# Four graph layers on one core: the column lists of layer 0 made tile by tile, more listed tiles there, and three edge sums moved to layer 2

## The chip, the cores and the metric

One Trainium2 chip, of which the kernel uses one core. The metric is device time in microseconds of one execution, given as the median of several runs. Before the change the three runs took 2618.31, 2622.95 and 2624.23 us, so the median is 2622.95.

## What is computed

The inputs are node features x (4096 x 256) and an adjacency matrix adj (4096 x 4096, float32), whose entries thin out towards high row and column numbers: entry (i, j) is non-zero with a probability that falls with the square root of i times j, and the diagonal is full. Four layers follow one another, each with a residual and a layer norm:

```python
x = ln(x + adj @ (x * W))                 # layer 0
x = ln(x + L1(x, adj))                    # layer 1: two steps of top-p attention beside R = rownorm(adj + I)
x = ln(x + L2(x, adj))                    # layer 2: softmax of adj * score over the neighbours, times x
neighbour_edges = einsum('ij,ji->i', adj, adj)
x = ln(x + concat(x, adj @ x, neighbour_edges) @ weight + bias)   # layer 3
```

The edge sum of layer 3 for a row i, the sum over j of adj[i, j] * adj[j, i], depends on adj alone, so it can be worked out at any time before layer 3.

## The kernel before

**Tiles.** There are 32 row tiles of 128 rows. Rows of low number have neighbours nearly everywhere, so tiles 0 to 2 (DENSE = 3) are always multiplied with all 32 column blocks. For the others the kernel finds which columns of adj hold anything for the tile, and makes a list of these columns, in blocks of 128. CAPS (line 66) says how many blocks each tile's list may have: 7, 7, 6, 7, 5, 6, 5, 5, 5, 5, 5, 5, 6 for tiles 3 to 15, then 5 for eight tiles and 4 for eight, 146 in all. A listed block costs a gather of 128 rows by GpSimd (an indirect DMA, line 393), wherever it is used: features in each of the layers, and once the pair of adj and its transpose, 128 rows of 256 numbers.

**Layer 0** (its pieces from line 476, its loop from line 619). SyncE's queue loads the whole adjacency, 256 KB panels for tiles 0 to 15 (dense_0, line 547) and 512 KB parts for tiles 16 to 31 (find_0, line 560). VectorE reduces each of these to `seen` (lines 552 and 563), which says for each row and column block whether a column is used. TensorE multiplies the panels of tiles 0 to 15 with x (line 550). Once all of tiles 16 to 31 are seen, list_columns makes one list for all sixteen: eight lists of a sixteenth of the columns each, by rounds of MAX8 and MATCH_REPLACE (lines 347 and 349) over 512 elements. Then a tile is started every third turn (L_EVERY); listed_0 gathers its pairs and its rows of x, multiplies them (line 593), forms the edge products on VectorE (lines 595 and 402), and writes the blocks of the tile to HBM (pk) for later layers. The same loop slips in edges_0, the edge sums of tiles 0 to 2, from 2 MB loads on ScalarE's queue and products of 2048 columns (line 614). The end of a tile, out_0, is cut in seven pieces (rone, y, st, mv on VectorE, rs on GpSimd, xi on VectorE, transposes and projections on TensorE, copies and DMAs on ScalarE), and move_ends lets one piece go per turn, two apart from the tile ahead.

**Layer 1, first step.** A plan written out by hand (PERIOD and AT) orders the pieces of each tile's attention (narrow). It makes its own short lists of large attention weights, tile by tile (lines 1212 to 1254). Beside it r_stream multiplies the listed blocks with the layer's features: the tiles 16 to 31 first, whose blocks are in pk, then tiles 3 to 15, whose pairs have to be gathered here and whose edge products are formed here (line 1352). The second shared list, for tiles 3 to 15, is made here too. **Second step:** for each tile, a search on VectorE and ScalarE over 4096 attention weights (lines 781, 787, 862, 868, 910, 914), a dense product with the features (line 237), and the listed blocks beside it (line 1087).

**Layers 2 and 3** are two calls of product: the panels of the hub tiles (0 to 2 in layer 2, 24 panels; 0 to 5 in layer 3, 48) are mixed with the pieces of the listed tiles from 31 down. In each turn it fetches up to three pieces ahead (loads on SyncE's queue, gathers on GpSimd), weighs the piece of the next turn (ScalarE exponentials at line 1593 and a VectorE product at line 1594, in layer 2 only), multiplies this turn's piece (line 1659), and moves the ends of finished tiles by a step.

**Order.** Inside these parts the program's order on TensorE, ScalarE, VectorE and GpSimd is that of the code (`manual_schedule(engines=everything)`); SyncE's queue is ordered by the framework's scheduler. Each engine works its queue in order. If a check at the end finds that a list was too short or a threshold failed, a complete second way through all layers runs instead.

## Time and profile before

The profile is of one execution of 2627.68 us; the span from its first to its last instruction is 2625.9 us, with a mean granted TensorE clock of 0.933.

| engine | busy us | share of the span | instructions |
|---|---|---|---|
| TensorE matmul | 2197.5 | 84% | 10680 |
| VectorE | 2064.5 | 79% | 6152 |
| GpSimd | 1704.6 | 65% | 2778 |
| ScalarE | 1478.7 | 56% | 2413 |
| DMA, 16 engines | 392.17 MB, mean 149 GB/s | | |

| gathers at line 393 | count | mean ns | first and last start, us |
|---|---|---|---|
| pairs of adj, in layer 0 and the first step of layer 1 | 146 | 1033 | |
| x, layer 0 | 72 | 1024 | 231.5, 462.8 |
| qtab, layer 1, first step | 146 | 960 | 505.8, 1073.3 |
| ttab, layer 1, second step | 146 | 994 | 1269.7, 2191.8 |
| x2d, layer 2 | 146 | 1007 | 2242.7, 2433.1 |
| y3d, layer 3 | 126 | 964 | 2455.1, 2613.8 |

How to read it: "busy" is the time in which an engine had an instruction under way, so a share below 100% can still be a full queue if each instruction is followed by a gap that belongs to it. A group line gives the code line, engine, operation, output and inputs with shapes and count, then busy us and mean ns of one, then the idle time of the engine just before these instructions and what ended it. A stretch line gives the busy time of TensorE (matmuls, then weight loads), VectorE, ScalarE and GpSimd with instruction counts, then the granted clock, the mean busy share of the 16 DMA engines and GB/s. The shares are means over layers with different limits, so each layer has to be read by itself.

### The profile page before, as it was taken

The page shows a single profiled execution, that of the slowest core. Times are in us where ns is not written, and L with a number is a line of the kernel's source. Part 1 is how long each engine was busy: PE and PEld are TensorE (multiplying, and loading weights), DVE is VectorE, ACT ScalarE, POOL GpSimd, SP SyncE. Part 2 cuts the span into 40 slices and gives each one's busy share as a digit, 9 for nine tenths or more (in the row PEclk, how much of TensorE's full clock was granted, in tenths as well). Part 3 has the DMA queues.
Part 4 walks back from the last instruction along what each step waited for, and adds up shares of the span by engine and source line. Part 5 has one row for each costly group of instructions (what it writes and reads, how often), then busy time and mean ns, then how long its engine had stood idle before and what let it go on. Part 6 is the DMA issues. An engine that isn't in the chain of part 4 may idle for free.

```text
span 2625.9 us, 37696 instructions
## 1 busy us (share of the span) xinstructions
PE 2197.5 (84%) x10680; PEld 1572.6 (60%) x10680; DVE 2064.5 (79%) x6152; ACT 1478.7 (56%) x2413; POOL 1704.6 (65%) x2778
## 2 busy tenths in 40 slices
PE   6887789679988988869888888888888877798997
PEld 4666567336555555557666666666666666566774
DVE  5876455588899987366698999999999996677586
ACT  0000111258778877556688888888888982444100
POOL 1005877356666666524688888888888873677576
PEclk8999899779999989889999999999999998899997
DMA  9996977435545554635311111111111112777794
GB/s 311 350 313 224 322 229 226 131 117 165 159 139 150 149 143 140 209 116 178 111 56 49 57 47 45 53 50 48 48 47 44 54 36 77 237 227 223 238 300 156
DMA packets 261978, 392.17 MB, mean 149 GB/s; under 512 B 41920, under 2 KB 170320, under 8 KB 260992
## 3 DMA queue, kind: packets, MB, share of 16 engines
q1 hardware_dynamic: 160992, 203.82, 24.2%
q0 software_dynamic: 46112, 131.50, 17.3%
q10 hardware_dynamic: 54656, 54.35, 6.1%
q8 instruction: 88, 1.44, 0.2%
q14 instruction: 130, 1.06, 0.1%
HBM read 329.25 MB, written 60.26 MB: 148 GB/s over the span
## 4 chain that ended last, share of the span: by engine, by line
DVE 22%; PE 18%; POOL 7%; ACT 5%; issue 4%; DMA 2%; SPq 0%; POOLq 0%; DVEq 0%; ACTq 0%
PE psa L237 5%; PE acc L1659 5%; DVE cand L868 4%; DVE tmp L862 3%; PE acc L1087 2%; DVE e L914 2%; DVE top L845 2%; PE lg L671 2%; DVE rest L847 2%; ACT junk L781 2%; PE po L464 1%; POOL xg L393 1%; PE pt L226 1%; DVE e L910 1%; POOL shift L1015 1%
## 5 line engine op out<-in xcount | busy, mean ns | idle before, releaser
L237 PE MATMUL psa<-v,eT 128*128 128x256 f32 x2048 | 515.7, 400 | 81.6 <-ACT eT L228 81.6
L237 PEld LDWEIGHTS psa<-v,eT 128*128 128x128 f32 x2048 | 402.1, 200 | 162.8 <-ACT eT L228 105.9
L550 PE MATMUL acc<-xw,panel 128*128 128x257 f32 x1024 | 255.3, 399 | 38.7 <-DMA panel<-in_panels 25.7
L781 ACT ACTIVATE junk<-e,h 128x4096 bf16<-128x4096 f32 x64 | 237.4, 3710 | 52.1 <-POOL h L761 41.1
L550 PEld LDWEIGHTS acc<-xw,panel 128*128 128x128 f32 x1024 | 197.1, 199 | 96.6 <-issue 35.1
L226 PE MATMUL pt<-ident,e 128*128 128x128 f32 x1024 | 156.9, 283 | 90.4 <-DVE e L914 68.7
L787 ACT ACTIVATE junk<-e,h 128x4096 bf16<-128x4096 f32 x62 | 230.9, 3724 | 0.1
L226 PEld LDWEIGHTS pt<-ident,e 128*128 128x128 f32 x1024 | 129.7, 147 | 134.5 <-issue 82.5
L868 DVE MAX8 cand<-tmp 128x8 f32<-128x128 f32 x1024 | 203.8, 276 | 1.1
L248 ACT COPY xT<-ptx 128x256 f32<-128x256 f32 x96 | 35.8, 372 | 287.9 <-PE ptx L245 237.1
L228 ACT COPY eT<-pt 128x512 f32<-128x512 f32 x256 | 145.2, 591 | 90.5 <-PE pt L226 89.9
L393 POOL DMA_INDIRECT xg<-qtab,idx_x x146 | 140.1, 960 | 70.7 <-issue 32.5
L393 POOL DMA_INDIRECT pc<-in_pair,idx_a x146 | 150.8, 1033 | 50.1 <-issue 34.9
L393 POOL DMA_INDIRECT xg<-ttab,idx_x x146 | 145.1, 994 | 57.0 <-issue 28.5
L1167 DVE MAX8 cand<-e 128x8 f32<-128x256 f32 x512 | 175.9, 410 | 3.4 <-ACT e L1159 3.4
L393 POOL DMA_INDIRECT xg<-x2d,idx_x x146 | 147.1, 1007 | 46.7 <-issue 22.0
L1197 ACT ACTIVATE marks<-e,mid 128x1024 bf16<-128x1024 f32 x128 | 140.2, 1144 | 48.9 <-DVE mid L1193 40.8
L393 POOL DMA_INDIRECT xg<-y3d,idx_x x126 | 121.5, 964 | 59.2 <-DMA t3d<-t 21.1
L910 DVE SCALAR_TENSOR_TENSOR e<-e,ties 128x1024 f32<-128x1024 f32 x128 | 155.9, 1280 | 2.9
L1156 PE MATMUL lg<-kT,qi 64*128 64x512 f32 x512 | 154.7, 676 | 1.3 <-DVE qp L516 1.0
L464 PE MATMUL po<-u,xT 128*128 128x512 f32 x256 | 138.6, 669 | 20.3 <-DVE qp L516 19.8
L742 ACT ACTIVATE e<-lg 128x1024 f32<-128x1024 f32 x120 | 123.5, 1029 | 52.5 <-PE lg L671 52.5
(347 smaller groups left out, 5519.0 us busy)
## 6 DMA issues: line engine op xcount, KB each, us to landing
panel<-in_panels SPq DMA_DIRECT2D x200, 256.0 KB
e<-in_panels SPq DMA_DIRECT2D x64, 512.0 KB
pc<-pk SPq DMA_DIRECT2D x53, 320.0 KB
e<-in_hubs ACTq DMA_DIRECT2D x6, 2048.0 KB
xg<-ttab SPq DMA_DIRECT2D x96, 128.0 KB
pc<-pk SPq DMA_DIRECT2D x39, 256.0 KB
pc<-in_panels SPq DMA_DIRECT2D x32, 256.0 KB
tab<-xi ACTq DMA_DIRECT2D x33, 160.0 KB
```

What stands on the lines that cost most here:

```text
L226: nc.tensor.transpose(pt[:, k, :], e[:, (g * 4 + k) * P:][:, :P], ident)
L228: nc.scalar.copy(eT[g], pt)
L237: nc.tensor.matmul(ps[:, :D], eT[g][:, k, :], rhs[j][:, :D], start=(j == 0), stop=stop and j == NT - 1)
L393: nc.gpsimd.indirect_dma_start(out=o, out_offset=None, in_=src, in_offset=bass.IndirectOffsetOnAxis(ap=idx[:, c], axis=0))
L464: nc.tensor.matmul(po.rearrange("p a b -> p (a b)"), xT[:, h, :], u[:, h, :], start=(h == 0), stop=(h == 1))
L550: nc.tensor.matmul(ps[:, :D + 1], a[:, k, :], XW[j][:, :D + 1], start=(j == 0), stop=(j == NT - 1))
L781: nc.scalar.activation(junk_tile(), e, AF.Relu, bias=h, scale=-1.0, accum_out=part)
L787: nc.scalar.activation(junk_tile(), e, AF.Sign, bias=h, scale=-1.0, accum_out=below)
L868: nc.vector.max(cand[:, c * (NS // 2) + g, :], w[:, g * SEG:(g + 1) * SEG])
L910: nc.vector.scalar_tensor_tensor(eg, eg, ties[:, g:g + 1], eg, op0=OP.is_gt, op1=OP.mult)
L1156: nc.tensor.matmul(a["lg", c][:, k, :], a["qi"][r, :], kT[r, c * LC:(c + 1) * LC], start=True, stop=True)
L1167: nc.vector.max(a["cand"][:, b, :], a["e"][:, b * SEG0:(b + 1) * SEG0])
```

## The change

It has four parts.

1. **Lists tile by tile.** list_columns and its tables go. list_one makes an exact list of one tile: a scan over the 32 blocks for each row, four small matmuls that turn counts into offsets, a comparison of 128 to 896 slot numbers with these offsets, a matmul for each listed block, and ten small VectorE instructions that turn ranks into column numbers. It is the method that the first step of layer 1 uses already, whose constant tables are now made at the start.
2. **24 listed tiles in layer 0 instead of 16.** LE is 8 instead of 16: tiles 0 to 7 are multiplied densely and reduced panel by panel, tiles 8 to 31 are found in wide parts. The loop is new: a dense panel every second turn, six found parts in seven turns, a list started when a tile has been seen and three turns have passed (APART), and the tile's gathers as soon as its list is done, while the rest of adj is still loaded. Ends keep three apart instead of two. Tiles 3 to 7 keep their place in layer 1 for pairs and edge products, but their lists are made in layer 0.
3. **130 listed blocks instead of 146**, since exact lists need fewer slots: 7, 6, 6, 6, five of 5, twenty of 4.
4. **Edge sums of tiles 0 to 2** move from layer 0 to layer 2: edges_1 is stepped once in each turn of its product. It loads two parts of 512 KB on SyncE's queue in one turn and multiplies them on VectorE in the next, twelve times, in one pair of buffers (the idle half of kT).

The check for lists that are too short looks at each tile's count, with one compare and one reduce over `seen` more.

```diff
+F_SLOTS, APART = (6, 7), 3
-LE = P // NL
+LE = 8
-CAPS = (NT,) * DENSE + (7, 7, 6, 7, 5, 6, 5, 5, 5, 5, 5, 5, 6) + (5,) * 8 + (4,) * 8
+CAPS = (NT,) * DENSE + (7, 6, 6, 6) + (5,) * 5 + (4,) * 20
...
+    def list_one(I):
+        K, pool = CAPS[I], pools["lists"]
+        has = pool.tile([P, NT], F32, name="has", bufs=2)
+        nc.vector.tensor_scalar(has, seen[:, :, I], 0.0, None, op0=OP.is_gt)
+        upto = pool.tile([P, NT], BF16, name="upto", bufs=2)
+        nc.vector.tensor_tensor_scan(upto, ones.to_broadcast([P, NT]), has, 0.0, op0=OP.mult, op1=OP.add)
+        nc.vector.tensor_mul(ranks[I % 2][:, :NT], upto, has)
+        mine = upto[:, NT - 1:]
+        yield
+        pd = lists_ps[:, MOST:].rearrange("p a b -> p (a b)")[:, :NT + 4]
+        nc.tensor.matmul(pd[:, NT + 1:NT + 2], next_one, mine, start=True, stop=True)
...
+        nc.scalar.copy(rows_of[:, I, :], pd[:, NT + 2:])
+        step = pool.tile([P, NT + 2], BF16, name="step", bufs=2)
+        nc.scalar.copy(step, pd[:, :NT + 2])
+        yield
+        since = pool.tile([P, MOST * P], BF16, name="since", bufs=1)
+        nc.vector.tensor_scalar(since[:, :K * P], slots[:, :K * P], rows_of[:, I, 0:1], None, op0=OP.is_ge)
+        yield
+        pi = lists_ps[:, :MOST]
+        for k in range(K):
+            nc.tensor.matmul(pi[:, k, :NT + 2], since[:, k * P:(k + 1) * P], step, start=True, stop=True)
+        yield
+        nc.vector.tensor_sub(want, slot_1[:, :K], pi[:, :K, NT + 1])
+        nc.vector.tensor_reduce(most, ranked, AX.X, OP.max)
...
+        nc.vector.tensor_copy(idx_x[:, cols], want)
+        nc.vector.tensor_scalar(idx_a[:, cols], want, float(NT), float(I), op0=OP.mult, op1=OP.add)
...
-            if far - e[1] >= 2:
+            if far - e[1] >= 3:
...
+        while multiplying or finding or soon or later or active or listing or ends:
             move_ends()
+            if n % (NT // 2 // LE) == 0:
+                multiplying = next(dense, dense) is not dense
+            if finding and (found * F_SLOTS[1] <= n * F_SLOTS[0] or not multiplying):
+                finding = next(find, find) is not find
+                found += 1
             run_rest()
+            for g in list(active):
+                if next(g, g) is g:
+                    active.remove(g)
+            for I, g in list(listing):
+                if next(g, g) is g:
+                    listing.remove((I, g))
+                    if I >= LE:
+                        active.append(listed_0(I))
+            if (soon or later) and n - started >= APART:
+                listing.append(((soon or later)[0], list_one((soon or later).pop(0))))
+                started = n
+            n += 1
...
+    def edges_1():
+        part = small.tile([P, DENSE, 4], F32, name="part_e", bufs=1)
+        half = [kT[:, N // 2:][:, s * CC:(s + 1) * CC] for s in range(2)]
+        for I in range(DENSE):
+            for c in range(N // CC):
+                for t, h in zip(half, hubs):
+                    nc.sync.dma_start(t, h[rows(I), c * CC:(c + 1) * CC])
+                yield
+                nc.vector.scalar_tensor_tensor(half[0], half[0], 1.0, half[1], op0=OP.mult, op1=OP.mult,
+                                               accum_out=part[:, I, c:c + 1])
+                yield
+        nc.vector.tensor_reduce(edge[:, :DENSE], part, AX.X, OP.add)
...
                 multiply(t)
                 passed[chunks[t][2] is not None] += 1
+                next(beside, None)
...
-    product(0, x2d, D + 1, X2, panels_of, nbr_weights, end_2)
+    product(0, x2d, D + 1, X2, panels_of, nbr_weights, end_2, beside=edges_1())
```

## The prediction

> **What bounds the kernel now.** I read three views, in this order: the busy time of each engine by stretch of the span (PE, PEld, DVE, ACT, POOL, then granted clock, share of the DMA engines, GB/s), the instruction groups of single stages, and the instructions in order of time where one stage hands over to the next. The time order gives the seams: layer 0 runs from 0 to the first logits at 503.8 us, layer 1's first step to about 1079, its second step to the first gather of layer 2 at 2242.7, layers 2 and 3 to 2625.9.
>
> ```profile
> 50.00:100.00 50.00, 44.57 (x199) 34.39 (x198) 39.75 (x58) 4.44 (x15) 3.04 (x6) 1.00 0.98 342
> 100.00:150.00 50.00, 42.83 (x187) 32.49 (x186) 40.16 (x62) 2.96 (x10) 3.83 (x8) 1.00 0.99 348
> ...
> 250.00:300.00 50.00, 39.25 (x157) 28.34 (x156) 28.14 (x54) 5.45 (x20) 41.97 (x57) 0.86 0.85 284
> 300.00:350.00 50.00, 37.48 (x157) 28.18 (x155) 24.69 (x47) 5.88 (x21) 38.41 (x50) 0.86 0.86 276
> ...
> 800.00:850.00 50.00, 44.69 (x307) 27.45 (x307) 47.65 (x178) 41.58 (x77) 35.34 (x37) 1.00 0.54 154
> ```
>
> Layer 0 has two halves with different bounds. Up to 200 us the DMA share is 0.98, GpSimd idle. From about 230 us GpSimd is the bound: 42 of 50 us busy, and the 0.3 us "issue" gap after each gather fills the rest. Layer 1's first step (800 to 850) is bound by VectorE (47.65 of 50) with TensorE just behind.
>
> ```profile
> L552 DVE TENSOR_REDUCE seen<-panel 128x4 bf16<-128x512 f32 x128 | 87.1, 682 | 14.7 <-DMA panel<-in_panels 14.6
> L563 DVE TENSOR_REDUCE seen<-e 128x8 bf16<-128x1024 f32 x64 | 77.8, 1216 | 17.4 <-DMA e<-in_panels 17.1
> L393 POOL DMA_INDIRECT pc<-in_pair,idx_a x72 | 77.3, 1074 | 27.6 <-issue 17.5 <-DVE idx_a L370 8.0 <-DMA pc<-in_pair,idx_a 1.2
> ...
> L393 POOL DMA_INDIRECT xg<-in_x,idx_x x72 | 73.7, 1024 | 14.3 <-issue 13.4 <-DMA xg<-in_x,idx_x 1.0
> ```
>
> These are groups of layer 0. The gathers of 16 listed tiles run from 231.5 to 462.8 us, 14.5 us a tile, none before. The groups also give DVE idle that is no DMA wait: rone 57.3 and 24.5 us behind TensorE, qp 36.5 behind ScalarE, xi 28.0 behind GpSimd, 146 us in all over 32 tile ends.
>
> ```profile
> 2320.00:2340.00 20.00, 18.51 (x74) 13.15 (x73) 16.83 (x56) 9.33 (x30) 15.41 (x16) 1.00 0.71 210
> 2340.00:2360.00 20.00, 17.05 (x64) 11.69 (x63) 16.28 (x61) 7.80 (x26) 15.42 (x16) 0.91 0.72 209
> ...
> 2480.00:2500.00 20.00, 19.08 (x91) 16.23 (x91) 18.03 (x70) 0.00 (x0) 15.12 (x17) 1.00 0.92 302
> 2500.00:2520.00 20.00, 19.19 (x90) 16.57 (x89) 17.55 (x65) 0.00 (x0) 15.11 (x17) 1.00 0.93 316
> ```
>
> In layers 2 and 3, 15.4 of 20 us on GpSimd is a full queue: 16 gathers of 0.95 us and 16 gaps of 0.30. Layer 2 makes 146 gathers in 191.3 us (1.31 each), layer 3 makes 126 in 159.7 (1.267).
>
> **Layer 0, VectorE.** Built but not run, the change shows 64 panel reduces for 128 and 96 wide ones for 64 (160.3 us for 164.9: -5). Edge products of 100 blocks instead of 72: 20 tiles of 4 at 0.738 + 1.036 and 4 of 5 at 0.818 + 1.249 are 43.8 for 30.7: +13. The products of the three longest tiles leave, -15. The shared list with its 12 MAX8 and 11 replacements, its spreads and reduces leaves, about -29. In come 29 lists of 14 small instructions. Layer 1 makes the same ones per tile: 0.177, 0.228, 0.194, a threshold of 0.579 for 640 columns (0.48 for 512), then subtract 0.151, four operations on 128 to 160 elements at 0.3, five of 0.15: 3.3 us a list, 96 us. [...] The net is +60: 306 us of DVE up to 500 become about 366.
>
> **Layer 0, the other engines.** TensorE loses 8 dense tiles (255.3 / 16 = 16.0 us each, -128), gains 28 blocks at 0.526 and the lists' small matmuls (43): about 399 become 326. ScalarE gains two 0.2 us copies a list, 12 us, on an engine idle for over 80% here. GpSimd: 200 gathers at 1.27 instead of 144, plus 32 ends at 1.9, are some 315 to 330 us, but they start near 45 us instead of 231, so its queue would be done near 375 and is no longer the bound. DMA: adjacency 67.1 MB at 2.87 us/MB (44.78 MB took 80.3% of 160 us between 50 and 210), gathers 26.2 MB at 3.64, outputs 30.7 MB at 2.93, x 12 us: 390 us of the 16 engines, 395 by the same count before. So the bytes do not shrink: the 36 us of edge loads leave, 27 us of gathers come early. SP's queue, which no hand orders, now has small loads of layer 1 (qi, x0r, xin) among the panels; they wait for tile ends, and two tiles of panels are loaded ahead, so I price them at nothing; uncovered, they idle the transfer queue some 7 us each for four or five.
>
> **How long layer 0 gets.** Keep the first 50 us (22 of DVE) and about 22 us of last tile end. Between them 344 us of DVE run at some share. Row 50:100 has 0.80, layer 1's first step 443.2 of 500 = 0.886 between 500 and 1000, its second step 0.95. These give 502, 460 and 434 us; DMA alone would need 50 + 342 / 0.95 + 22 = 432. I take 463, by the row of the stage whose load is most alike (four engines full): **-41 us**; ends +2 below its present length and 70 below.
>
> **Layer 1.** The first step loses, on VectorE, the second shared list (20 us) and the edge products of 44 blocks (27.1 by rows for 74, so 16): 36 us, or 41 at a share of 0.886. TensorE loses 16 blocks at 0.69 and some small matmuls, 16 us, or 18 at its 90%. GpSimd loses 60 gathers of 1.25, which only matters if it is the bound, and it isn't once the others are. What is late next is TensorE, so I take **-28** between 18 and 41. The second step keeps VectorE at 95% and its instructions; 16 gathers and matmuls lie beside it: **-2**.
>
> **Layer 2.** 130 gathers instead of 146 at 1.31: 170 us, -21. But the moved edge sums come here: 24 loads of 512 KB on SP's queue and 12 VectorE products of 1024 columns (1.28 by the row of L910, 15 us). DMA share was 74.4% of 200 us = 149; less 16 gathers (0.457 each) and their blocks (3), plus 12.6 MB at 2.87 = 36: 175 us. [...] rows here never pass 0.93. 175 / 0.93 = 188: **-3** for the -21 that gather counts alone would give. Each product also waits for its 1 MB while the pe weights of the next turn and the tile ends queue behind it on VectorE, and TensorE waits for the weights. Two turns take about 6.5 us (57 turns in some 188), the megabyte 3 us alone, 6 at half of the engines, plus product, issue and landing, some 7 to 10: 0 to 42 us lost at worst, 0 to 21 gained. On SP's queue each pair of loads waits for the product before it, and later panels and blocks queue behind; SP already waits there once a turn for the t3d writes, so I price that at nothing, and without this cover it is part of the 42.
>
> **Layer 3.** 111 gathers for 126: 19 us by GpSimd, 9 by TensorE (0.59 a block), which is 19 of 20 us busy until 2580: **-15**. The longer final checks (a 1024-wide compare and reduce, a dozen small ones) lie at layer 1's end, +1 at most.
>
> **Sum.** 41 + 28 + 2 + 3 + 15 - 1 = 88. The profiled execution took 2627.7 us (span 2625.9), so 2540; the median of the three runs stands 4.7 below it, so **2535 us**.
>
> **Rivals.**
> A, likeliest (0.55): as summed, 2535, its own range 2505 to 2565.
> B (0.22): layer 0's coupled queues hold VectorE at the 0.80 of rows 50 to 200. Layer 0 stays at 502, the rest gives 47: 2574. For it: each listed tile needs list, gather, matmul, product in order, through four in-order queues. Against: that 0.80 stood beside a DMA share of 0.98.
> C (0.13): layer 0 at 434 and the edge sums hidden: 70 + 28 + 2 + 21 + 15 - 1 = 135, so 2488. For it: the second step runs at 0.95. Against: there DMA is nearly idle.
> D (0.07), slower: VectorE keeps all 146 us of its waits on the other engines in layer 0, now beside more work: 50 + 344 + 146 + 22 = 562, +58, less 47: 2634. For it: gathers of one tile now run between the reduces of the next, on the same queue. Against: much of the 146 was slack under a GpSimd bound. It decides from 135 us of kept waits; I count with 45.
> E (0.03): B with the worst of the edge loads (-9 to +42 there), within a few us of 2619.
>
> A measurement can tell about 0.2% from no change, 5 us. Faster is A, B, C and some of E: 0.92; within 0.2%, 0.03; slower, 0.05. The range 2485 to 2590 reaches from C's centre past B's, and leaves out D, E and the half of C below.
>
> **What would show it.** Right: first pair gather near 45 us, first logits near 463, DVE above 0.85 from 100 to 400; the `mid` instructions of layer 1 at 15.3 us each for 16.2; DMA share above 0.9 in the first half of layer 2; 1.26 us between gathers in layer 3. Wrong: rone, xi or the edge product waiting more than 100 us in sum in layer 0; the products on hub columns idle before for over 20 us; layer 1's period unchanged.

## The result and the profile after

The changed kernel takes 2593.55 us (median of four, 2587.75 to 2599.38) beside 2620.63 for the kernel before on the same chip: ratio 0.9896, 95% interval 0.9868 to 0.9923. A second set of runs gave 0.9861 (0.9836 to 0.9887). So it is faster by some 27 to 36 us, where 88 were forecast, and the time lies just above the forecast's range. The seams between the stages, read as before from the order in time, say where:

| stage, us | before | after | moved | forecast |
|---|---|---|---|---|
| layer 0, to the first logits | 503.8 | 514.9 | +11.1 | -41 |
| layer 1, first step | 575.7 | 530.2 | -45.5 | -28 |
| layer 1, second step | 1163.2 | 1147.3 | -15.9 | -2 |
| layer 2 | 212.4 | 231.4 | +19.0 | -3 |
| layer 3 and end | 170.8 | 162.2 | -8.6 | -15, +1 for the final checks |
| span | 2625.9 | 2586.0 | -39.9 | -88 |

First the busy times by stretch, for the stretches that were shown of before (columns: PE, PEld, DVE, ACT, POOL, granted clock, DMA share, GB/s).

```profile
50.00:100.00 50.00, 32.69 (x144) 22.60 (x142) 35.70 (x83) 4.14 (x17) 33.70 (x53) 0.86 0.93 312
100.00:150.00 50.00, 38.75 (x173) 28.53 (x172) 41.93 (x100) 7.13 (x29) 32.68 (x51) 0.86 0.93 301
250.00:300.00 50.00, 34.87 (x143) 24.28 (x141) 34.49 (x85) 6.65 (x28) 28.45 (x43) 0.80 0.84 266
300.00:350.00 50.00, 33.09 (x141) 23.34 (x142) 40.41 (x97) 6.60 (x27) 23.44 (x37) 0.81 0.75 240
...
800.00:850.00 50.00, 47.63 (x324) 28.80 (x325) 45.04 (x181) 42.23 (x86) 30.84 (x33) 1.00 0.57 146
```

Layer 0 no longer has two halves: gathers run from 45 us on, beside everything else. But no engine is full any more. VectorE, which was to be at 44 of 50 us, has 34 to 42, TensorE 33 to 39 at a granted clock of 0.80 to 0.86 where it had 0.86 to 1.00, GpSimd 23 to 34, and the DMA share falls from 0.93 to 0.75. In the row of layer 1's first step VectorE has 45.0 for 47.7 and TensorE 47.6: TensorE has become the fuller one there, as the forecast said.

The groups of layer 0 after:

```profile
L531 DVE TENSOR_REDUCE seen<-e 128x8 bf16<-128x1024 f32 x96 | 115.9, 1214 | 19.1 <-DMA e<-in_panels 19.1
L371 POOL DMA_INDIRECT pc<-in_pair,idx_a x100 | 99.8, 998 | 117.9 <-issue 40.7 <-DVE idx_a L358 38.0 <-PE lists_ps L332 12.7
L371 POOL DMA_INDIRECT xg<-in_x,idx_x x100 | 97.5, 974 | 18.0 <-issue 16.9 <-DMA pc<-in_pair,idx_a 0.2 <-DMA xb<-xb 0.2
...
L521 DVE TENSOR_REDUCE seen<-panel 128x4 bf16<-128x512 f32 x64 | 43.5, 681 | 3.3 <-DMA panel<-in_panels 3.3
```

The work is about what was counted: 159.4 us of reduces (160.3 forecast), 200 gathers, VectorE 354 us up to 500 (366 forecast). The amounts were right, the time that they take was not.

Layers 2 and 3 after (20 us rows, same columns):

```profile
2250.00:2270.00 20.00, 18.37 (x64) 11.55 (x64) 15.21 (x45) 8.03 (x27) 9.44 (x10) 0.93 0.85 265
2270.00:2290.00 20.00, 12.93 (x42) 8.74 (x41) 14.13 (x46) 5.76 (x20) 11.43 (x11) 0.84 0.89 291
2480.00:2500.00 20.00, 18.80 (x86) 15.90 (x86) 17.69 (x62) 0.00 (x0) 15.12 (x17) 1.00 0.94 305
2500.00:2520.00 20.00, 16.63 (x78) 14.31 (x77) 17.58 (x66) 0.00 (x0) 15.13 (x17) 1.00 0.93 296
```

In layer 3 GpSimd's 15.1 of 20 us is the same full queue as before, only over 111 gathers. In layer 2 the 15.4 of 20 is gone: 10 or 11 gathers in 20 us for 16, while the DMA share has gone up from 0.71 to 0.85 and 0.89. The hub columns of the edge sums are being loaded there.

### The profile page after: what moved, and what is told of

It is laid out like the page before. It is cut to its first block, busy times and chain, and to the rows that moved or that the text cites. A ratio compares the mean times of both kernels' runs of the same rounds, so it can differ in the third digit from the quotient of the medians.

```text
span 2586.0 us, 36948 instructions
## 1 busy us (share of the span) xinstructions
PE 2087.2 (81%) x10252; PEld 1483.9 (57%) x10252; DVE 2091.6 (81%) x6401; ACT 1475.9 (57%) x2455; POOL 1631.2 (63%) x2720
## 4 chain that ended last, share of the span: by engine, by line
DVE 25%; PE 16%; ACT 7%; issue 5%; POOL 4%; DMA 3%; SPq 0%; DVEq 0%; ACTq 0%; POOLq 0%
PE acc L1621 5%; PE psa L235 4%; DVE cand L830 4%; DVE e L876 3%; DVE tmp L824 3%; DVE e L872 3%; PE acc L1059 2%; ACT junk L743 2%; DMA kT<-in_hubs 2%; PE lg L633 2%; DVE top L807 2%; DVE rest L809 2%; ACT junk L749 1%; PE pt L224 1%; ACT e L704 1%
## 5 line engine op out<-in xcount | busy, mean ns | idle before, releaser
L235 PE MATMUL psa<-v,eT 128*128 128x256 f32 x2048 | 504.0, 393 | 75.0 <-ACT eT L226 74.5
L749 ACT ACTIVATE junk<-e,h 128x4096 bf16<-128x4096 f32 x62 | 230.8, 3723 | 0.1
L371 POOL DMA_INDIRECT pc<-in_pair,idx_a x130 | 129.0, 992 | 128.4 <-issue 48.6
L371 POOL DMA_INDIRECT xg<-x2d,idx_x x130 | 134.6, 1036 | 69.2 <-PE acc L1621 31.0
L519 PE MATMUL acc<-xw,panel 128*128 128x257 f32 x512 | 156.1, 458 | 25.4 <-DMA panel<-in_panels 14.1
L1150 ACT ACTIVATE marks<-e,mid 128x1024 bf16<-128x1024 f32 x128 | 140.5, 1145 | 39.9 <-DVE mid L1146 35.8
L371 POOL DMA_INDIRECT xg<-ttab,idx_x x130 | 128.7, 990 | 52.8 <-issue 27.5
L371 POOL DMA_INDIRECT xg<-qtab,idx_x x130 | 125.6, 966 | 54.7 <-issue 30.9
L824 DVE SCALAR_TENSOR_TENSOR tmp<-e,h 128x2048 f32<-128x2048 f32 x64 | 150.8, 2356 | 2.3
L1109 PE MATMUL lg<-kT,qi 64*128 64x512 f32 x512 | 148.1, 653 | 3.0 <-DVE want L356 2.9
L519 PEld LDWEIGHTS acc<-xw,panel 128*128 128x128 f32 x512 | 116.0, 235 | 58.2 <-issue 32.9
L633 PE MATMUL lg<-kT,qi 64*128 64x512 f32 x480 | 135.5, 641 | 15.6 <-ACT junk L707 15.6
L371 POOL DMA_INDIRECT xg<-y3d,idx_x x111 | 106.6, 960 | 63.7 <-PE acc L1621 41.5
```

What stands on the lines that cost most here:

```text
L235: nc.tensor.matmul(ps[:, :D], eT[g][:, k, :], rhs[j][:, :D], start=(j == 0), stop=stop and j == NT - 1)
L371: nc.gpsimd.indirect_dma_start(out=o, out_offset=None, in_=src, in_offset=bass.IndirectOffsetOnAxis(ap=idx[:, c], axis=0))
L519: nc.tensor.matmul(ps[:, :D + 1], a[:, k, :], XW[j][:, :D + 1], start=(j == 0), stop=(j == NT - 1))
L633: nc.tensor.matmul(ps[:, h, :], qi[r, :], kT[r, (n * NC + c) * LC:][:, :LC], start=True, stop=True)
L749: nc.scalar.activation(junk_tile(), e, AF.Sign, bias=h, scale=-1.0, accum_out=below)
L824: nc.vector.scalar_tensor_tensor(w, ec, h, ec, op0=OP.is_lt, op1=OP.mult, accum_out=low[:, c:c + 1])
```

## The experiments

Eighteen runs, each one to four edits away from the changed kernel; e16 is the changed kernel itself. The stages come from one profile each (us; the last column is the ratio of the median time to that of before on the same chip, with its 95% interval). Each run comes with what was expected of it before it ran; the letters in the text behind it are the theories named there.

| run | layer 0 | L1 first | L1 second | layer 2 | layer 3 | ratio |
|---|---|---|---|---|---|---|
| after | 514.9 | 530.2 | 1147.3 | 231.4 | 162.2 | 0.9896 (0.9868-0.9923) |
| e16, after again | 516.8 | 526.2 | 1148.3 | 230.2 | 160.6 | 0.9861 (0.9836-0.9887) |
| e1, 16 listed | 522.2 | 533.8 | 1148.4 | 230.5 | 159.0 | 0.9917 (0.9887-0.9947) |
| e2, no hub edges | 525.8 | 530.3 | 1147.7 | 200.3 | 160.7 | 0.9765 (0.9745-0.9784) |
| e3, 146 blocks | 555.5 | 529.1 | 1162.7 | 235.4 | 170.3 | 1.009 (1.007-1.011) |
| e4, no edge products | 512.9 | 530.7 | 1148.8 | 229.3 | 160.4 | 0.984 (0.9809-0.9871) |
| e5, 117 turns | 509.3 | 529.3 | 1144.8 | 230.8 | 158.4 | 0.9819 (0.9788-0.985) |
| e6, qp later | 518.6 | 526.1 | 1147.8 | 227.1 | 160.5 | 0.9879 (0.9849-0.9909) |
| e7, ScalarE's order | 504.8 | 530.3 | 1147.6 | 230.4 | 158.4 | 0.9762 (0.9744-0.978) |
| e8, half of po | 515.8 | 530.9 | 1149.0 | 230.3 | 160.2 | 0.9852 (0.9829-0.9876) |
| e13, edges in tail | 527.4 | 530.4 | 1144.9 | 200.0 | 159.9 | 0.9778 (0.9749-0.9806) |
| e14, GpSimd relieved | 511.5 | 529.7 | 1145.1 | 230.6 | 159.1 | 0.9843 (0.982-0.9865) |
| e15, all four | 504.4 | 528.4 | 1145.0 | 199.7 | 160.2 | 0.967 (0.964-0.97) |
| e17, e15 less e14 | 505.7 | 530.1 | 1148.1 | 201.9 | 159.0 | 0.97 (0.9678-0.9723) |
| e18, wait of 7 | 495.5 | 532.1 | 1149.7 | 227.5 | 158.7 | 0.9751 (0.9728-0.9773) |
| e9, two pairs | 537.1 | 765.8 | 1148.5 | 239.4 | 189.5 | 0.9724 (0.9687-0.9761) |
| e11, pace and order | 515.3 | 774.2 | 1150.2 | 248.0 | 187.9 | 0.9698 (0.9663-0.9732) |
| e12, e9 and e11 | 515.1 | 773.1 | 1146.0 | 239.1 | 191.8 | 0.9659 (0.9614-0.9704) |
| e10, fewer gathers | 512.4 | 770.0 | 1150.4 | 248.0 | - | - |

After, e16 and e2 have the same layer 0 and show 514.9, 516.8 and 525.8: a single profile tells nothing there below some 11 us, and the ratios decide. The other stages repeat within 4 us. The last four rows are from a chip on which the first step of layer 1 took 766 to 774 us and layer 3 took 188 to 192. They are compared with one another only, and not by their ratios: the kernel before lost more on that chip (2972.5 us for some 2623) than the changed one with two pairs did (e9: 2883.65).

### How much listing in layer 0 is worth: e1

```diff
-LE = 8
+LE = 16
```

> The changed kernel with 16 listed tiles in layer 0 instead of 24 (LE = 16), all else as changed; so 8 more tiles take the dense panels in layer 0 and have their weights gathered in layer 1. The loop of layer 0 makes 136 turns in both settings. Theory A (handoffs: layer 0 is a fixed number of turns, and a turn's length is set by results handed between four engines, each in a fixed order): first logits at 500 to 520 us, as with 24, so the eight extra listed tiles buy nothing in layer 0, and all that they buy is in layer 1, first step 20 to 35 us longer than the changed kernel's 530; whole time 2610 to 2630. Theory B (amount of work: what VectorE, the DMA queues and TensorE have to do sets layer 0): 24 listed tiles take 256 panel matmuls of 0.4 us from TensorE but put 8 tiles' products and gathers on VectorE and GpSimd; with VectorE the bound, layer 0 becomes 15 to 30 us shorter with 16, at 485 to 500, and layer 1 loses about as much; whole time 2590 to 2605.

Layer 0 522.2, 2 us past A's range, and ratio 0.9917: some 5 to 15 us above the changed kernel's 0.9861 to 0.9896, with intervals that overlap. Layer 1's first step lost 3.6 us, not 20 to 35. So the eight further listed tiles are worth little, in layer 0 about as A says, and in layer 1, where neither theory said it. What holds the changed kernel's layer 0 is not learned from this run, for it ends against another limit: from 400 to 500 us TensorE is busy without a gap with the dense panels that are left.

```profile
400.00:500.00 100.00, 100.00 (x502) 81.38 (x501) 59.39 (x168) 13.52 (x54) 19.61 (x34) 0.98 0.59 179
```

### Which engine's work holds layer 0: e4, e8, e14

```diff
-        es = es_tile()[:, 0, :]
+        es = zero_es
...
-            pr = pools["gat"].tile([P, PIECE, P], F32, name="pr", bufs=2)
-            nc.vector.tensor_mul(pr[:, :b - a, :], pc[:, :b - a, 0], pc[:, :b - a, 1])
-            add_up(es, pr[:, :b - a, :], m)
```

> The changed kernel without the edge products of the 24 listed tiles in layer 0 (their edge sums are left out of the output): 24 multiplications and 24 sums on VectorE, 17.1 + 25.6 = 42.7 us, are not done; no turn, gather, matmul or tile's end is taken out. Theory A (handoffs over 136 turns): the freed time turns into waits of VectorE, and the first logits come 0 to 15 us earlier, at 500 to 515. Theory B (VectorE's amount of work): 35 to 43 us earlier, at 472 to 480. The other stages as in the changed kernel, so the whole time is 2580 to 2594 by A, and 2550 to 2560 by B.

512.9: A. The forecast's core, that VectorE's amount of work sets layer 0, falls here. What became of the freed time is in VectorE's waits from 60 to 460 us, first after, then e4 (sum in us, times, longest). rone is the first instruction of a tile's end, which needs the sums that TensorE makes last; qp is VectorE's last one there, which needs ScalarE's copy qs:

```profile
DVE rone L449 <- PE acc L566: 39.6, 16, 6.3
DVE qp L485 <- ACT qs L480: 30.6, 18, 4.9
```

```profile
DVE rone L449 <- PE acc L566: 56.3, 18, 8.9
DVE qp L485 <- ACT qs L480: 50.1, 20, 6.4
```

VectorE was busy 305.8 us of these 400 after and 271.1 in e4, 34.7 less; these two waits are 36.2 longer. In this profile all of it was given back, at the places where VectorE stands for TensorE and ScalarE. By the ratio, 0.984, some 5 to 15 us of the whole may be kept, which the intervals hardly tell from nothing.

```diff
-        po = times_both(xT, U[0])
+        po = bank([P, 2, D], "po", "ms")
+        nc.tensor.matmul(po.rearrange("p a b -> p (a b)"), xT[:, 0, :], U[0][:, 0, :], start=True, stop=True)
```

> The changed kernel with half of one product left out: in layer 0 the product of a tile's features with U1 takes only the first 128 of its 256 features, so the output is not the reference's. That takes 64 matmuls of 0.75 us, 48 us with their gaps about 55 us, from TensorE, which has 355 us busy in layer 0's 515, and leaves every handoff in place. Theory P (TensorE is the link that every turn waits for): first logits 35 to 50 us earlier, at 465 to 480. Theory S (ScalarE's queue): 0 to 10 us earlier, at 505 to 515. Theory N (no engine alone): part of it, 10 to 25 us, at 490 to 505.

515.8, ratio 0.9852: TensorE's amount of work isn't it either. The row of 40 to 460 us, before, after and e8:

```profile
40.00:460.00 420.00, 351.05 (x1540) 268.32 (x1541) 271.03 (x504) 42.42 (x151) 201.16 (x314) 0.93 0.85 281
```

```profile
40.00:460.00 420.00, 297.46 (x1267) 213.05 (x1266) 320.63 (x780) 49.25 (x208) 242.46 (x366) 0.83 0.83 269
```

```profile
40.00:460.00 420.00, 284.67 (x1204) 208.59 (x1203) 320.46 (x780) 49.12 (x207) 239.17 (x361) 0.79 0.83 268
```

The product's own group fell from 79.4 to 46.1 us, 33, but TensorE's busy time only by 13: its clock went from 0.83 to 0.79, and a dense matmul from 458 to 481 ns (399 in the kernel before, at 0.93). The changed kernel's own profiles show 0.81 to 0.83 here (after, e16, e2), so 0.79 lies just below their scatter: TensorE, with less to do, did it somewhat more slowly.

```diff
-            nc.gpsimd.memset(xs[-1][:, D:], 1.0)
+            nc.vector.memset(xs[-1][:, D:], 1.0)
...
-        nc.gpsimd.tensor_add(xb, xi[:, :D], bb)
+        nc.vector.tensor_add(xb, xi[:, :D], bb)
```

> The changed kernel with two of GpSimd's side jobs in layer 0 given to VectorE: the addition of the bias to a tile's features (32 of 795 ns, 25 us) and the writing of the ones beside each gathered block (100 of 122 ns, 12 us). GpSimd keeps its gathers and the two small steps of each norm; VectorE gets about 14 + 8 = 22 us of work more. Theory G (GpSimd's queue of gathers is what layer 0 waits for most): first logits 20 to 35 us earlier, at 480 to 500, although VectorE, the engine that the forecast took for the bound, has more to do. Theory N (no engine alone): within 8 us of the changed kernel. Theory V (VectorE is the bound after all, and its waits hid it): 10 to 20 us later.

511.5, ratio 0.9843 beside e16's 0.9861 in the same set of runs: N. Neither taking 37 us from GpSimd nor putting 17 us on VectorE is seen; that the two cancel each other is not excluded, for TensorE's wait for gathered rows was 30.1 us where it was 23.1.

### The number of turns: e5

```diff
-F_SLOTS, APART = (6, 7), 3
+F_SLOTS, APART = (1, 1), 3
...
-            if n % (NT // 2 // LE) == 0:
+            if n % 5 in (0, 2, 4):
```

> The changed kernel with the same work of layer 0 in 117 turns of its loop instead of 136: a quarter panel of a dense tile in three of five turns instead of one of two, and a quarter of a listed tile's panel to be searched in every turn instead of six of seven. Not one instruction is added or taken away. Theory A (a turn has a length of its own, 515 / 136 = 3.8 us, set by handoffs): 19 turns fewer make layer 0 about 60 us shorter, first logits at 445 to 465, whole time 2525 to 2550. Theory B (the amount of work sets the time): the turns become longer by as much as they become fewer, first logits at 500 to 515, whole time 2580 to 2594.

509.3, near B: the turns became longer, from 3.8 to 4.35 us, almost as much as they became fewer. The ratio of 0.9819 says some 11 to 20 us of gain, with an interval that overlaps e16's. A turn has no length of its own.

### The handoffs: e6, e7, e18

```diff
+        yield
         last_of_slot.append(rest)
         yield
```

> The changed kernel with VectorE's last operation of each tile's end (qp, line 485) one turn later, so that ScalarE's copy that it needs has been done for a turn: the wait of 51 us in sum that VectorE spends there, with all its queue behind it, goes. No work is added. Theory A (handoffs set the length of a turn): with the largest of the handoff waits gone, most of it comes off layer 0 unless the next one in the same turn takes its place: first logits at 470 to 500 if half or more is kept, whole time 2550 to 2580. Theory A2 (the waits in a turn are one loop through all engines, so a wait removed at one place appears at another): 508 to 518, with VectorE's wait for the sums (line 449) or for the panels longer by what the other lost. Theory B (amount of work on another engine or on the DMA queues is the bound): as A2 in time, but with one of these resources above 0.95 busy in the stretch from 100 to 400 us.

518.6, ratio 0.9879: A2, just past its range. The wait for qs fell from 30.6 to 6.6 us (60 to 460), the one of rone rose from 39.6 to 55.0. B asked for a resource above 0.95 from 100 to 400 us; in the rows of 40 us from 80 to 400 the DMA share was 0.86 in the mean, with 0.98 in one row, and VectorE's 245 of 320 us the most of any engine, so B is not borne out.

What stands ahead of qs on ScalarE is seen in the changed kernel's instructions in order of time (start, duration, engine; ACTq is a transfer that ScalarE issues; in brackets the idle time before and what ended it):

```profile
208.16 0.96 ACTq L475 DMA_DIRECT2D tab<-xi  x1
...
209.17 0.44 ACTq L476 DMA_DIRECT2D tak<-xi  x1
...
209.65 0.44 ACTq L477 DMA_DIRECT2D tak<-xi  x1
210.19 0.40 ACTq L478 DMA_DIRECT2D xb<-xb  x1
...
210.63 0.37 ACT L480 COPY qs<-po 128x256 f32<-128x256 f32 x1 [2.50 <-DMA tab<-xi]
...
211.03 0.48 DVE L485 SCALAR_TENSOR_TENSOR qp<-po,rone,qs 128x256 f32<-128x256 f32 x1 [3.83 <-ACT qs L480]
211.44 0.82 DVE L338 TENSOR_SCALAR since<-slots,rows_of 128x512 bf16<-128x512 f32 x1
...
212.32 0.29 PE L342 MATMUL lists_ps<-step,since 128*128 128x34 bf16 x4 [3.64 <-ACT xT L246]
```

Four transfers are issued in 2.5 us by an engine that the page calls idle; the copy comes behind them, VectorE stands 3.83 us for the copy, the next list's comparison (since) behind that, and TensorE 3.64 us before the matmul that takes the comparison. One late step on the emptiest engine holds three queues.

```diff
+        qs = pool.tile([P, D], F32, name="qs")
+        nc.scalar.copy(qs, po[:, 1, :])
         nc.scalar.dma_start(tab[rows(I), :], xi)
...
-        qs = pool.tile([P, D], F32, name="qs")
-        nc.scalar.copy(qs, po[:, 1, :])
...
+        yield
         nc.scalar.copy(edge[:, I:I + 1], ps[:, D + 1:D + 2])
```

> The changed kernel with two changes of order on ScalarE's queue in layer 0 and no other: the copy of qs, which VectorE waits for, comes ahead of the four writes of a tile's end that ScalarE issues (0.4 to 1.0 us each in the trace) instead of behind them, and the copy of a listed tile's edge sum with the writes of its blocks comes one turn later, where the profile had ScalarE waiting 103 us for VectorE. Theory S (ScalarE's queue, 62 us busy by the profile's count but with some 130 us of issuing writes that it doesn't count, is the link that every turn waits for): first logits 20 to 50 us earlier than the changed kernel's 515, at 465 to 495. Theory P (TensorE's part of a turn sets it): within 6 us of 515. Theory N (no engine alone: four queues coupled by results that are handed over one turn later, so that time won on one is lost on the next): 505 to 515.

504.8 by its profile, which was the slowest of its four runs, 9.6 us above their median; ratio 0.9762, clear of the changed kernel's: 26 to 35 us. The profile's 504.8 alone would be N; by the ratio it is S, at the near end of its range, and by order alone. VectorE's wait for qs is down to 11.3 us; the one for the sums (rone) is 60.0 for 39.6, so part of it was again given back.

The run holds two edits and was not taken apart. The second one took away the larger wait, that of ScalarE for VectorE at the edge sum's copy (up to 500 us, after and e7):

```profile
ACT edge L568 <- DVE y L452: 115.4, 23, 21.5
```

```profile
ACT edge L569 <- DVE y L452: 20.0, 14, 5.9
```

As e6 had cut the wait for qs as far by another way, and gained nothing, the later copy of the edge sum may well be the part that counts. That is not shown.

```diff
-L_EVERY, L_WAIT = 3, 5
+L_EVERY, L_WAIT = 3, 7
```

> The changed kernel with the matmuls of a listed tile two turns later behind its gathers (L_WAIT 7 for 5) and nothing else. In the changed kernel TensorE stands 23 us in sum before these matmuls until a gather has landed and 10 us more without a shown reason, with a dense panel and the next tile's list behind it. Theory G2 (that landing, not GpSimd's work, is what made the blocks cost 1.7 us a gather): the wait is gone, layer 0 at 490 to 505, ratio 0.977 to 0.984. Theory N: the wait is gone and layer 0 stays at 508 to 520, ratio 0.985 to 0.990, with VectorE's or TensorE's waits on the other handoffs longer. A tile's last end comes two turns later by either, 7 us at most.

495.5, ratio 0.9751: G2. TensorE's longest waits up to 500 us, after and e18 (acc L561 are the matmuls of a listed tile, psq and ptx the projections and transposes of a tile's end, lists_ps those of the next list):

```profile
PE psq L292 <- ACT xT L246: 24.6, 15, 4.5
PE acc L561 <- DMA xg<-in_x,idx_x: 23.1, 14, 6.8
PE ptx L243 <- DVE xi L464: 22.6, 8, 6.6
```

```profile
PE ptx L243 <- DVE xi L464: 51.5, 16, 7.7
PE lists_ps L329 <- DVE want L356: 39.0, 10, 7.2
```

The wait for the gathers' landing is gone (from TensorE's list altogether), and though the waits for VectorE doubled, 19 us of layer 0 and 29 to 38 us of the whole by ratio were kept. The ratio, 0.9751, is even below the range that was given for G2.

### The blocks and the gathers: e3, e10

```diff
-CAPS = (NT,) * DENSE + (7, 6, 6, 6) + (5,) * 5 + (4,) * 20
+CAPS = (NT,) * DENSE + (7, 7, 7, 7, 6) + (5,) * 16 + (4,) * 8
```

> The changed kernel with 146 listed blocks, as many as before, shared out so that no tile from 8 on has more than 5: 16 more blocks, 12 of them in layer 0. Theory A (the blocks make layer 1's gain, as forecast, by more than was forecast): layer 1's first step goes back from 530 to 565 to 576 us, its second step from 1147 to 1155 to 1163, layer 2 is 15 to 20 us longer (16 gathers of 1.26 us) and layer 3 too; whole time 2650 to 2680. Theory B (layer 1's first step gained by the eight tiles that need no gathered weights there, or by lists made in another order): first step within 10 us of 530, second step within 5 of 1147; whole time 2610 to 2630. In layer 0, 24 gathers of 1.26 us more on GpSimd move the first logits by 0 to 10 us by either.

Of A, the second step (1162.7), layer 3 (170.3) and the whole (2651.26 us) hold; the first step (529.1) is B; and layer 0 at 555.5, 30 to 41 us above the three profiles of the changed kernel's layer 0, is neither. 24 gathers of 1.26 us are 30, so here they seem to count in full; but the twelve blocks also bring their matmuls, edge products and longer lists.

```diff
-        for k in range(CAPS[I]):
+        for k in range(CAPS[I] - 1):
             xs.append(pools["gat"].tile([P, D + 1], F32, name="xg", padded_shape=[P, D + 2]))
...
+                nc.tensor.matmul(ps[:, :D + 1], pc[:, min(k, CAPS[I] - 2), 1], xs[min(k, CAPS[I] - 2)], start=(k == 0), stop=(k == CAPS[I] - 1))
```

> The changed kernel with one of the four (or five) gathers of features of each listed tile in layer 0 left out, its matmuls taking the tile before it again, so the output is not the reference's. 24 gathers of 0.97 us, 1.26 us with the gap behind each, 30 us on GpSimd; turns, matmuls, VectorE's and ScalarE's work are as before. Only the time to the first logits counts here. Theory G (the gathers are on the path of layer 0: twelve blocks more made it 41 us longer, 1.7 us for each gather): first logits at 475 to 495. Theory N (no engine alone; the blocks' matmuls, lists and products made the 41 us together): 500 to 512.

Behind layer 3 this kernel goes through the program's fallback with all columns, so only its layer 0 is read: 512.4 beside 537.1 of e9, whose layer 0 is the changed kernel's, on the same chip. About 25 us for 24 gathers: G by size, though from one profile each, where the same layer 0 has scattered by 11 us. With e14 and e18 the reading is: the gathers are on the path less by GpSimd's time than by when the last of a tile lands, since TensorE stands for it.

### The edge sums: e2, e9, e13

```diff
-    product(0, x2d, D + 1, X2, panels_of, nbr_weights, end_2, beside=edges_1())
+    product(0, x2d, D + 1, X2, panels_of, nbr_weights, end_2)
+    nc.vector.memset(edge[:, :DENSE], 0.0)
```

> The changed kernel without the edge sums of tiles 0 to 2 in layer 2: their 24 loads of 0.5 MB and 12 products on VectorE are left out, and the output lacks these sums. Theory A (the loads and products in layer 2 are what made it 19 us longer instead of the 3 us shorter that were forecast: a product waits up to 6.8 us for its loads and holds the weights behind it on VectorE): layer 2 falls from 231 to 205 to 213 us, the rest unchanged, whole time 2568 to 2576. Theory B (the turn of layer 2 is longer for another reason, such as tiles with fewer blocks and so more ends for as many gathers, and the edge work lies beside gathers that set the time anyway): layer 2 at 222 to 231, whole time 2584 to 2594.

Layer 2 200.3 and ratio 0.9765: past A. The sums cost 31 us, and 16 fewer blocks had saved 12 (212.4 to 200.3). One turn of the changed kernel in order of time shows the waiting part (SPq is the load's issue):

```profile
2208.01 0.39 SPq L1567 DMA_DIRECT2D kT<-in_hubs  x1
2208.08 0.68 DVE L1542 SCALAR_TENSOR_TENSOR pe<-panel,pe 128x512 f32<-128x512 f32 x1
...
2215.05 1.23 DVE L1569 SCALAR_TENSOR_TENSOR kT<-kT 128x1024 f32<-128x1024 f32 x1 [6.28 <-DMA kT<-in_hubs]
2216.20 0.08 DVE L1569 DVE_READ_ACCUMULATOR kT<-kT 128x1 f32 x1
2216.20 0.70 DVE L1542 SCALAR_TENSOR_TENSOR pe<-pc,pe 128x512 f32<-128x512 f32 x1
...
2216.95 2.00 PE L1621 MATMUL acc<-xg,pe 128*128 128x257 f32 x8 [3.31 <-DVE pe L1542]
```

The megabyte takes 7 us from its issue, VectorE stands 6.28 us with the product at its head, the weights of the next turn come behind it, and TensorE 3.31 us behind the weights. The bytes show in the rows of the first 100 us of layer 2, first after, then e2:

```profile
2192.00:2242.00 50.00, 33.91 (x118) 25.31 (x118) 25.43 (x67) 20.29 (x65) 38.31 (x38) 0.87 0.95 306
2242.00:2292.00 50.00, 36.31 (x118) 24.27 (x119) 38.25 (x126) 15.79 (x52) 28.43 (x27) 0.83 0.87 275
```

```profile
2204.00:2254.00 50.00, 43.49 (x165) 32.43 (x166) 34.29 (x113) 23.85 (x77) 38.12 (x40) 0.91 0.80 236
2254.00:2304.00 50.00, 43.66 (x169) 30.35 (x168) 43.31 (x154) 24.42 (x80) 38.42 (x39) 0.97 0.80 237
```

Without the loads the stretch has room for 334 matmul instructions instead of 236.

```diff
-        half = [kT[:, N // 2:][:, s * CC:(s + 1) * CC] for s in range(2)]
+        quarter = [kT[:, s * CC:(s + 1) * CC] for s in range(4)]
+        pairs = [quarter[2:], quarter[:2]]
...
+            if k + 1 < len(parts):
+                load(k + 1)
+            yield
+            yield
+            a, b = pairs[k % 2]
+            nc.vector.scalar_tensor_tensor(a, a, 1.0, b, op0=OP.mult, op1=OP.mult, accum_out=part[:, I, c:c + 1])
+            yield
+            yield
```

> The changed kernel with the edge sums of tiles 0 to 2 in layer 2 spread out: two pairs of 0.5 MB buffers (all of kT instead of its second half) and one product in four turns, four turns behind its loads, instead of one pair and one product in two turns, one turn behind its loads. The same 24 loads and 12 products. Without any of this work layer 2 took 200 us for the changed kernel's 231. Theory A (the 31 us are waiting: a product stands first on VectorE until its megabyte has landed, 26 us in sum, and holds the weights that TensorE needs): layer 2 falls to 203 to 212, whole time 2565 to 2578. Theory B (the 31 us are the bytes: 12 MB more at about 300 GB/s is 40 us of all queues in a stage that takes 200, so gathers and panels come later whenever they are loaded): layer 2 at 222 to 232, whole time 2585 to 2594.

On its chip layer 2 takes 239.4 (e12 239.1) with two pairs and 248.0 (e10 and e11) with one. VectorE's waits for the loads are gone (16.3 us in e11, none in e9), and 9 us with them. If the sums cost as much on this chip as on the others, the greater part of the 31 stays, as B has it: the 12.6 MB themselves. The stage without the sums was not run there, and the chip's unexplained waits in layer 2 ("remote", on VectorE 18.5 us in e9 and 6.4 in e11) are as large as the 9 us, so the shares of waiting and bytes are no more than a reading.

```diff
+    def edges_0():
+        part = small.tile([P, DENSE, 4], F32, name="part_e", bufs=1)
...
+            a, b = pairs[k % 4]
+            nc.vector.scalar_tensor_tensor(a, a, 1.0, b, op0=OP.mult, op1=OP.mult, accum_out=part[:, I, c:c + 1])
+            if k + 3 < len(parts):
+                load(k + 3)
+            yield
...
+            if not finding:
+                next(hub_edges, None)
```

> The changed kernel with the edge sums of tiles 0 to 2 taken out of layer 2 and put back into layer 0, into its last 24 turns: the same 24 loads of 0.5 MB and 12 products, into the two tiles that the search of panels no longer needs, one product in each turn, three turns behind its loads. In the changed kernel the DMA queues are 0.45 to 0.65 busy there and VectorE about half. Theory A (the sums cost layer 2 31 us because its stretch is full, by bytes and by waits, and would cost little where queues and VectorE are idle): layer 2 at 198 to 204, layer 0 at 514 to 526, whole time 2563 to 2575. Theory B (layer 0 is as sensitive to what is added, as the twelve more blocks' 41 us suggest): layer 2 at 198 to 204, but layer 0 at 535 to 550, whole time within 6 us of the changed kernel's.

Layer 2 200.0, layer 0 527.4, ratio 0.9778 beside 0.9861: A. The same bytes and products in the last turns of layer 0, where the DMA share had been 0.45, cost 2 to 13 us there by the profiles and save 31 in layer 2; by the ratios 22 us are kept.

### Together: e11, e12, e15, e17, e16

> The changed kernel with two of the changes already measured alone put together: the work of layer 0 in 117 turns instead of 136, and ScalarE's copy of qs ahead of the writes with the edge sum's copy a turn later. Alone the first gave about 20 us of the whole time and the second about 35. Theory A (both take away waits of different links, and what one leaves is not what the other takes): first logits at 460 to 485, whole time 2535 to 2555. Theory B (they take away the same wait, or each is followed by the same next link): no better than the better of the two, first logits at 490 to 500, whole time 2560 to 2570.

On its chip layer 0 is 515.3, 22 us below e9's 537.1 with the changed kernel's layer 0. By scale that is no more than e7's gain alone on the other chips, so whether pace adds to order stays open.

> The same two changes in layer 0 and the edge sums in layer 2 with two pairs of buffers. If the stages are independent, the time is that of the kernel with the first two less what the third gains alone: by theory A of both, 2510 to 2535; by theory B of both 2560 to 2570.

Layer 0 as e11 (515.1 for 515.3), layer 2 as e9 (239.1 for 239.4): the stages are independent, by one profile each. The absolute times expected don't apply to this chip; the median, 2869.0 us, is below e11's 2878.56 and e9's 2883.65.

> All together: 117 turns, ScalarE's order, GpSimd's side jobs on VectorE, and the edge sums in the last turns of layer 0. If the gains add up as measured alone (35 + 20, then 20 to 35, then 20 to 30), the whole time is 2475 to 2510 on a chip on which the kernel before takes 2622. If layer 0 comes to a floor of its own work first (VectorE's 362 us of operations in it, with 37 us more, would fill 400 of 450), 2500 to 2530.

2541.93 us (2534.47 to 2545.42), ratio 0.967: faster than both kernels, by 84 us than before. But it is above either range: of 50 us against e16, 22 are e13's, so pace, order and relief together give some 28 us, no more than order alone. Gains in layer 0 do not add up.

> 117 turns, ScalarE's order and the edge sums in the last turns of layer 0, but GpSimd keeps its side jobs (the version with all four took 0.967 of the kernel before, its layer 0 504 us). Theory N (no engine alone: in the shorter turns VectorE has become as full as the others, 37.7 of 50 us, so 22 us of additions on it cost more than GpSimd gains): layer 0 at 490 to 502, ratio 0.958 to 0.965. Theory G (GpSimd's queue is the link that counts): layer 0 at 508 to 525, ratio 0.968 to 0.976.

Layer 0 at 505.7 lies between the ranges of N and G; the ratio of 0.97 is in G's, but its interval overlaps e15's. So neither is decided, and e14's edit can't be told from nothing in the shorter turns either.

> The changed kernel once more, as it is, beside the others on their chip: for the scatter of its stages between two profiles. Layer 0 at 510 to 527, layer 1's two steps at 530 and 1147, layer 2 at 231, layer 3 at 160, each within 4 us but layer 0, and the ratio to before at 0.987 to 0.992. If the ratio lies outside, the comparisons across calls are good to no better than that.

As expected but for a ratio a little lower than the range; the whole times of different sets of runs compare to about 0.3% (0.9896 and 0.9861).

## Why the prediction was wrong

**Layer 0 (forecast -41, measured +11): the step that failed.** "I take 463, by the row of the stage whose load is most alike (four engines full)". The work was counted about right; the share of VectorE was carried over from layer 1's first step, 0.886, and came out at 320.6 / 420 = 0.76 between 40 and 460 us. The prediction's own sum, 50 + 344 of work + idle time + 22, had room for 45 us of idle time; between 50 and 493 us VectorE worked 327 us and stood for 116, of which 95 were waits for the three other engines (rone 46.9, qp 39.4, xi 8.4). So rival B described layer 0 (502 us), and its 2574 was the nearest; rival E, B with the edge loads at their worst, also had the sign of layer 2, and the measured time lies between the two. Rival D's mechanism, waits kept beside more work, went two thirds of its way.

The prediction's own rows gave B too little weight. "Up to 200 us the DMA share is 0.98" does not hold for the last of them, and what was said against B, that VectorE's 0.80 "stood beside a DMA share of 0.98", falls with it: in the kernel before, VectorE had the same 0.80 from 150 to 200 us, at a DMA share of 0.84.

```profile
150.00:200.00 50.00, 43.09 (x216) 33.43 (x216) 39.79 (x67) 3.85 (x13) 3.75 (x7) 0.97 0.84 288
```

But a sum over one engine was the wrong form: e4 took 35 us of work out of it, and it grew 36 us of waits. What the runs put in its place: four queues in fixed order, whose results are handed over one turn later, none of the engines fuller than 0.84 in any 50 us of the changed kernel's profile (0.86 in e16's). Two changes of order alone shortened it by taking waits away: the landing of a tile's gathers before its matmuls (e18, and e3 and e10 by size), and ScalarE's place behind VectorE and behind the writes that it issues (e7, its two edits not separated). The rest of layer 0 isn't resolved link by link. e18 with e7 wasn't tried, and the spacing of the tiles' ends, three apart where it had been two, was in no run put back.

The DMA share was 0.90 to 0.95 from 50 to 250 us, so the loads of adj are a rival for that half. The trace speaks against them. Behind the first 50 us neither TensorE nor VectorE stands for a panel or a found part (0.5 us in sum up to 250 us, before weight loads). It is SyncE's queue that stands, 88 us in these 200, until VectorE has read a panel and its buffer is free. What the two engines do wait for is gathers (50 to 250 us):

```profile
PE acc L561 <- DMA xg<-in_x,idx_x: 15.8, 8, 6.8
```

```profile
DVE pr L563 <- DMA pc<-in_pair,idx_a: 4.6, 1, 4.6
```

```profile
SPq L516 <- DVE seen L521: 88.0, 17, 10.6
```

Whether the high share makes these gathers land later was not tested. Behind 250 us, with the share falling from 0.84 to 0.45, nothing is full: no engine has more than 40.4 of 50 us.

"each listed tile needs list, gather, matmul, product in order" stood in the prediction, as a rival's argument with a chance of 0.22. It should have had a price. TensorE's clock also went down, 0.93 before and 0.83 after, while its busy time from 40 to 460 us fell from 351 to 297 us, a loss that no term held.

**Layer 1, first step (-28, measured -45.5).** The sign and the `mid` spacing were right, 14.9 us for 15.3. The size wasn't: "GpSimd loses 60 gathers of 1.25, which only matters if it is the bound". In the kernel before, the step's 380 gathers at 0.97 us and a gap of 0.30 are 483 us of the 502 between its first and last `mid`; after, 320 are 406. So it was close to a bound. That is argued, not shown: more blocks alone (e3, 340 gathers) and more dense tiles alone (e1, 356) leave the step at 529 and 534. What neither run brings back is the making of the second shared list in this step, which is so a likely place of the gain; the rest together, near that bound, is another. No run put the list back.

**Layer 1, second step (-2, measured -16).** "16 gathers and matmuls lie beside it" failed: with 146 blocks (e3) the step is at 1162.7 again, before's 1163.2. VectorE, busy 90% from 1200 to 2000 us and 95% from 2000 to 2200 in the kernel before, didn't hide them; 16 blocks cost 15.4 us of the step, about 1 us each.

**Layer 2 (-3, measured +19).** The mechanism was named, but two terms were mis-sized: the edge sums cost 31 us, where -3 beside -21 had left 18 for them (42 at worst), and the 16 blocks saved 12, where 21 were counted. The sign named for being right came in part (DMA share 0.95 in the first quarter, 0.88 over the first half), the one named for being wrong in full (the hub products idle for 26.4 us). By e9 perhaps a third is waiting and the rest bytes in a stage whose DMA share is high; that split is open. SyncE's queue, on which the loads were issued, did not hide the bytes: in the stage's first 100 us the DMA share was 0.95 and 0.87 with them and 0.80 without (e2).

**Layer 3 (-15, measured -9)**: right in mechanism (1.265 us between gathers; e3, with 125 of them, is at 170.3 again), high in size, nearer to the 9 us that TensorE's count gave.

**The list's instructions**: 29 lists took about 100 us on VectorE, 96 forecast from rows of layer 1, so the rows held. The lists' smallest operations, on 128x4 elements, took 145 to 180 ns each, their threshold on 128x512 elements 556.

In sum, by spans 48 of the 88 us are missing: layer 0 52, layer 2 22 and layer 3 5, of which layer 1 gave 31 back. By medians it is 61, since the profiled execution of after was the fastest of its four and that of before lay 7 us above its median. That the time came within 4 us of the range is luck: it rests on these 31 us of layer 1, which were not forecast.

## What to carry to other kernels

A share of busy time didn't carry from one stage to another (VectorE's 0.886 in layer 1, 0.76 in layer 0): where several engines pass results round in fixed orders and none is full, price the handoffs (what is queued ahead of the result that others stand for), and don't expect work taken from any one engine to show. Try order first: two copies moved on one engine's queue (one ahead of the writes that it issues, one a turn later), or a consumer two turns later behind its gathers, gave 26 to 38 us here without an operation less, where 35 us of work removed from VectorE gave some 5 to 15 us, which the intervals hardly tell from nothing. Work that is moved "beside" a stage brings its bytes with it: here the same loads and products cost least where the DMA share was low (0.45 in layer 0's tail, 2 to 13 us in e13), and 31 us in layer 2 (e2), where the share in rows of 50 us had been 0.71 to 0.77 in the kernel before.

## What the runs showed of the hardware

- TensorE's granted clock went with the part of the time that it was busy. From 40 to 460 us it was busy 351 us at 0.93 in the kernel before, 334 at 0.89 in e1, 297 at 0.83 after, 285 at 0.79 in e8; the same dense matmul took 399, 408, 458 and 481 ns. So 33 us less work for it in e8 was 13 us less busy time. The busy time isn't all of it: with 296 to 298 us busy the clock was 0.80 in e3, 0.81 in e2, 0.82 in e4 and 0.83 after and in e6.
- Issuing a transfer from ScalarE held its queue for 0.40 to 0.96 us in the turn shown (0.33 to 1.5 over layer 0), and none of it counts as busy: an engine shown at 12% was the one that others stood for.
- One chip ran layer 1's first step in 766 to 774 us for 530 and layer 3 in 188 to 192 for 158 to 162, while the second step was not touched (1146 to 1150). In the first step the operations took about as long as elsewhere (a logits matmul 589 ns at the median, VectorE's MAX8 411 ns for 410), and several engines had idle time that the profile puts down to "remote". What it was isn't known.
